# Where three kinds of products stand among the scores of a step: doubled sums, mixing values and the MLP output, in a six-layer attention stack

## Chip, cores and metric

The kernel runs on one core of a Trainium2 chip. The metric is the device time of one launch in microseconds (us), the median of several runs.

## What is computed

Eight sequences of 512 rows and 128 features go through a layer norm, six attention layers with weights of their own, and a gated feed-forward network. Cut to what matters:

```python
def layer(h, p):
    q = (h @ wq.T + bq).reshape(bh, sl, H, DH)      # H = 16 heads of DH = 8
    k = (h @ wk.T + bk).reshape(bh, sl, H, DH)
    scores = einsum('blhd,bmhd->bhlm', q, k) / sqrt(DH)
    w_avg = softmax(scores).mean(axis=heads)        # averaged over the heads
    new_w = softmax(w_avg + rel)                    # rel: decay with distance
    sa = einsum('blm,bme->ble', new_w, h)           # mixes the rows of h themselves
    h1 = ln1(h + sa); h2 = ln2(h1)
    ff = relu(h2 @ w1.T + b1) @ w2.T + b2
    return ln3(h2 + ff)
x = x + six_layers(layernorm(x))
x = x + gated_ffn(layernorm(x))
```

## The kernel before

A **unit** is one layer of one sequence; there are 48, walked in order (line 798). A unit has 32 **steps** (line 810), numbered through the whole run as s = 32 x unit + step. Each step makes two score tiles of 128x512: `scores` (line 436) issues two matmuls on TensorE (line 445), VectorE takes the negated maximum of each row (`top`, line 454), and ScalarE takes the exponential with the row's sum accumulated (line 461). Two steps make a `Group` of four score tiles; eight steps cover one block of 128 query rows (`lc`) with all sixteen heads.

Everything else is placed among the steps by a plan written by hand: `at(step, place, fn)` (line 653) puts a function into the list of a step and a place, `first` in front of that list, and the main loop (lines 798 to 824) takes them out in the order: the two scores, then the list PE_, the two maxima, the lists DVE_ and ACT_, the two exponentials, and last the list RING_. Each engine works its instructions in the order in which they are issued here. The other work, with its steps:

- **Doubled sums** (`gather`, matmul line 483): sixteen small matmuls add the exponentials of two groups, weighted by 1/sum (`weights`, line 468: a reciprocal on VectorE, the product `rp` on GpSimd), into the PSUM tile `acc`. Planned five steps behind the second of the two groups (line 748), which gives steps 0, 4, 8, 12 and so on, first in PE_. After every second of them ScalarE takes `w = exp(acc / 16)` (`mix_exp`, line 491).
- **Mixing**: three steps later `mix_turn` transposes w (line 217, tile pt_w) and VectorE multiplies by the decay (`mix_decay`, line 501); two steps after that `mix_values` (line 506) multiplies by h into `po`, and VectorE's `mix_end` (lines 517 and 518) divides and adds h into `z1`. These are steps 7 and 9 of each eight, that is 7, 15, 23, 31 and 1, 9, 17, 25.
- **Projections** of the unit after (`project_k` at step 3, `project_q` at step 5, line 702), hidden products of the MLP of the unit two before (`hidden`, steps 11, 13, 19, 21), and transposes of h and u (steps 27 and 29). `matmuls` (line 665) puts the product into PE_ and what empties it on ScalarE into ACT_ of the same step, in front of the exponentials.
- **MLP output** (`mlp_out`, line 398): two halves of sixteen recorded matmuls each, in RING_ of steps 30 and 38 (6 of the next unit); `mlp_add` on VectorE a step later; the third norm's statistics at 32, 40 and its end from 41 on. One unit near the end has steps 26 and 30 instead.

[...] six of the pool `ps_big` (tag "big", taken in turn by `ring`, line 179) for the score tiles and the MLP output; one for `acc`; and one, of the pool `ps_one` (tag "one", line 176), that pt_w, po, pk, pq, pf, pt_h and pt_u all take in turn. A buffer's next writer waits until the last reader of the tile before has done.

## Time and profile before

| what | value |
|---|---|
| median of 3 runs | 2744.67 us (2743.7 to 2747.99) |
| the profiled execution | 2744.88 us, its span 2743.1 us |
| granted TensorE clock | 0.997 |
| busy: PE, VectorE (DVE), ScalarE (ACT), GpSimd (POOL) | 95%, 90%, 91%, 66% |
| exponentials (line 461) | 3072, the first at 25.6 us, the last at 2518.4 us |
| one unit in the middle of the run | 51.84 us (1007.86 to 1059.70) |
| feed-forward tail behind the last unit | 223 us (2520 to 2743) |

The profile is of one execution. A line of its groups gives the source line, the engine, the operation, output<-inputs with their shapes, the count, then the busy time and the mean of one in ns, and behind the second bar the idle time of that engine just before such instructions with what ended it. A line of its waits reads "who waits <- for whom: us in total, times, the longest". A line of its timeline gives start and length in us, engine, line, operation and tiles; "x16" is a burst of sixteen, and brackets hold the idle time before it with its releaser. A wait that overlaps the tail of the instruction before it isn't booked as idle, so starts are compared as well.

### The profile page before, as it was taken

The numbers are of one execution on the slowest core, as the hardware profiler recorded it, in microseconds if no ns is written. First come the engines' busy times: TensorE is split into PE (matmuls) and PEld (weight loads), VectorE is DVE, ScalarE is ACT, GpSimd is POOL, SyncE is SP. The second block draws the span as 40 slices with busy tenths as digits, with TensorE's granted clock in tenths as the row PEclk, the third lists the DMA queues.
The fourth block names the chain that finished last, engine by engine and source line by source line (L and its number), as shares of the span: only waits on it lengthen the run. The fifth ranks groups of instructions, "written<-read, shape, count | busy, mean of one in ns | idle before, by whom it ended". The sixth has DMA issues, their size and how long they took to land.

```text
span 2743.1 us, 50487 instructions
## 1 busy us (share of the span) xinstructions
PE 2592.6 (95%) x14944; PEld 1422.5 (52%) x14944; DVE 2461.5 (90%) x5725; ACT 2509.0 (91%) x6846; POOL 1815.7 (66%) x1894
## 2 busy tenths in 40 slices
PE   6999999999999999999999999999999999998999
PEld 3444555554554554554554554555554454455787
DVE  6999999999999999999999999999999999998774
ACT  6999999999999999999999999999999999998443
POOL 5567667667667667667667667657666756765874
PEclk9999999999999999999999999999999999999999
DMA  6445444354354454444444444444444545441000
GB/s 145 110 109 125 95 111 104 89 115 116 91 116 99 93 116 111 99 113 93 103 109 108 108 105 96 108 103 114 108 99 108 124 108 127 113 108 39 8 24 17
DMA packets 135847, 273.67 MB, mean 100 GB/s; under 512 B 39696, under 2 KB 57232, under 8 KB 135568
## 3 DMA queue, kind: packets, MB, share of 16 engines
q1 hardware_dynamic: 133504, 269.31, 42.2%
q8 instruction: 121, 1.98, 0.3%
q10 hardware_dynamic: 2064, 1.08, 0.2%
q14 instruction: 158, 1.29, 0.1%
HBM read 13.86 MB, written 2.10 MB: 6 GB/s over the span
## 4 chain that ended last, share of the span: by engine, by line
ACT 47%; PE 28%; DVE 16%; issue 5%; POOL 4%; SPq 1%; DMA 0%; POOLq 0%; DVEq 0%; ACTq 0%
ACT e L461 40%; DVE top L454 10%; PE acc L483 7%; PE ps L445 7%; PE qh L569 4%; PE py L404 3%; ACT g L394 3%; ACT w L491 2%; PE pk L260 2%; PE po L509 2%; PE pq L269 1%; ACT uT L382 1%; PE fo L615 1%; PE q L569 1%; DVE z L518 1%
## 5 line engine op out<-in xcount | busy, mean ns | idle before, releaser
L461 ACT ACTIVATE e<-ps,top 128x512 f32<-128x512 f32 x3072 | 2088.2, 728 | 97.2 <-DVE top L454 72.7
L454 DVE TENSOR_REDUCE top<-ps 128x1 f32<-128x512 f32 x3072 | 1930.5, 679 | 181.7 <-PE ps L445 179.9
L445 PE MATMUL ps<-ks,qs 128*128 128x512 f32 x3040 | 1187.4, 471 | 46.1 <-ACT e L461 34.7
L445 PEld LDWEIGHTS ps<-ks,qs 128*128 128x128 f32 x3040 | 521.0, 189 | 653.9 <-ACT e L461 440.8
L461 ACT ACTIVATION_READ_ACCUMULATOR e<-ps,top 128x1 f32 x3072 | 757.4, 247 | 0.0
L483 PE MATMUL acc<-e,rp 128*32 128x512 f32 x6144 | 740.5, 600 | 5.0 <-POOL rp L472 5.0
L472 POOL TENSOR_TENSOR rp<-pick,r 128x256 f32<-128x256 f32 x384 | 236.3, 615 | 598.3 <-DVE rw L517 226.8
L483 PEld LDWEIGHTS acc<-e,rp 128*32 128x32 f32 x6144 | 160.5, 109 | 349.1 <-issue 323.3
L315 POOL TENSOR_TENSOR m<-hiq,mask 128x512 f32<-128x512 f32 x190 | 241.0, 1278 | 0.1
L315 POOL TENSOR_TENSOR m<-loq,mask 128x512 f32<-128x512 f32 x190 | 241.1, 1279 | 0.0
L392 PE MATMUL pf<-uT,w 128*128 128x512 f32 x384 | 203.4, 611 | 27.6 <-DVE z L518 27.5
L509 PEld LDWEIGHTS po<-h,wT 128*128 128x128 f32 x1536 | 201.8, 192 | 21.2 <-DVE wT L501 3.4
L404 PE MATMUL py<-w,g 128*128 128x128 f32 x1536 | 191.7, 278 | 21.3 <-ACT e L461 21.3
L509 PE MATMUL po<-h,wT 128*128 128x129 f32 x1536 | 203.6, 276 | 3.0 <-DVE wT L501 3.0
L404 PEld LDWEIGHTS py<-w,g 128*128 128x128 f32 x1536 | 179.6, 191 | 47.2 <-ACT e L461 44.2
L279 POOL TENSOR_TENSOR loq<-qT,hiq 128x512 f32<-128x512 f32 x48 | 61.6, 1282 | 212.1 <-DVE hiq L278 212.1
L394 ACT ACTIVATE g<-pf,b_col 128x512 f32<-128x512 f32 x192 | 135.6, 706 | 1.5 <-PE pf L392 1.1
L501 DVE TENSOR_TENSOR wT<-pt_w,decay 128x512 f32<-128x512 f32 x192 | 130.7, 681 | 0.0
L217 PE MATMUL pt_w<-ident,w 128*128 128x128 f32 x768 | 120.4, 279 | 7.6 <-ACT uT L382 0.2
L491 ACT ACTIVATE w<-acc 128x512 f32<-128x512 f32 x192 | 118.0, 614 | 2.6 <-PE acc L483 2.4
L217 PEld LDWEIGHTS pt_w<-ident,w 128*128 128x128 f32 x768 | 88.0, 140 | 47.5 <-ACT g L394 36.1
L392 PEld LDWEIGHTS pf<-uT,w 128*128 128x128 f32 x384 | 65.3, 189 | 70.5 <-PE ps L445 53.6
(115 smaller groups left out, 2516.4 us busy)
## 6 DMA issues: line engine op xcount, KB each, us to landing
qs<-m SPq DMA_DIRECT2D x1520, 128.0 KB, 2.4
ks<-hik SPq DMA_DIRECT2D x384, 64.0 KB, 2.0
ks<-lok SPq DMA_DIRECT2D x376, 64.0 KB, 2.0
rows<-in_rows SPq DMA_DIRECT2D x6, 448.0 KB, 4.9
x_in<-in_x SPq DMA_DIRECT2D x8, 256.0 KB, 3.0
fh<-square SPq DMA_DIRECT2D x8, 256.0 KB, 2.3
x_out<-in_x SPq DMA_DIRECT2D x8, 256.0 KB, 2.8
out<-y SPq DMA_DIRECT2D x7, 256.0 KB, 2.4
```

What stands on the lines that cost most here:

```text
L217: nc.tensor.transpose(pt[:, c * P : (c + 1) * P], src[:, c, :], ident)
L315: nc.gpsimd.tensor_tensor(m[:, lc - 2 * two], part.unsqueeze(2).to_broadcast([P, NB, PER_STRIP, QB]), mask.unsqueeze(1).to_broadcast([P, N ...
L392: nc.tensor.matmul(pf, w1[:, f * P : (f + 1) * P], self.uT, start=True, stop=True)
L394: return lambda: nc.scalar.activation(self.g[:, f, :], pf, AF.Relu, bias=cols["b1_col"][:, k : k + 1])
L404: nc.tensor.matmul(self.py[:, k, :], self.g[:, f, c * P : (c + 1) * P], w2[:, f, :], start=(f == 0), stop=(f == FC - 1),)
L445: nc.tensor.matmul(ps[s], qs[:, nb * P : (nb + 1) * P].bitcast(F32R), un.ks[:, i, :].bitcast(F32R), start=True, stop=True,)
L454: nc.vector.tensor_reduce(top[s], ps[s], AX.X, ALU.max, negate=True)
L461: nc.scalar.activation(self.e[:, nb, :], ps[s], AF.Exp, bias=top[s], accum_out=self.zs[:, i % 2, nb : nb + 1],)
L472: nc.gpsimd.tensor_tensor(self.rp.rearrange("p t n l -> p (t n) l"), pick.unsqueeze(1).to_broadcast([P, 2 * NB, QB]), r.rearrange("p t n - ...
L483: nc.tensor.matmul(acc[nb * QB : (nb + 1) * QB, :], self.rp[:, gr.turn % 2, nb, :], gr.e[:, nb, :], start=(gr.turn == 0), stop=(gr.turn == ...
L491: nc.scalar.activation(self.w.rearrange("p c l -> p (c l)"), acc, AF.Exp, scale=1.0 / H)
L509: nc.tensor.matmul(self.po, self.wT[:, c, :], self.unit.h[:, c, 0 : E + 1], start=(c == 0), stop=(c == LC - 1),)
```

## The change

`mlp_out` and `mlp_add` now work on one quarter (128 rows) instead of a half. `scores` takes a function that it calls between its two matmuls; the list BETWEEN_ of a step is taken out there, and RING_ is gone. Three things go into BETWEEN_: the doubled sums, at the same steps as before; the mixing values, one step later (2, 10, 18, 26), with `mix_end` behind the maxima of that step; and the quarters of the MLP output, at steps 27, 30, 31 and 39, each with its addition in DVE_ of the same step. The third norm's first statistics move from 32 to 33. Nothing is added to or taken from the sum of products.

```diff
-        def mlp_out(self, half):
+        def mlp_out(self, c):
             w2 = lay[self.d][2]
-            self.py = ring([P, 2, E], f"py_{self.n}_{half}")
-            for k in range(2):
-                c = 2 * half + k
-                for f in range(FC):
-                    nc.tensor.matmul(
-                        self.py[:, k, :], self.g[:, f, c * P : (c + 1) * P], w2[:, f, :],
-                        start=(f == 0), stop=(f == FC - 1),
-                    )
+            self.py = ring([P, E], f"py_{self.n}_{c}")
+            for f in range(FC):
+                nc.tensor.matmul(
+                    self.py, self.g[:, f, c * P : (c + 1) * P], w2[:, f, :],
+                    start=(f == 0), stop=(f == FC - 1),
+                )
...
-        def mlp_add(self, half):
-            part = self.z3[:, 2 * half : 2 * half + 2, :]
-            nc.vector.tensor_tensor(part, self.py, part, ALU.add)
+        def mlp_add(self, c):
+            nc.vector.tensor_tensor(self.z3[:, c, :], self.py, self.z3[:, c, :], ALU.add)
...
-        def scores(self, half):
+        def scores(self, half, between):
...
                     un.ks[:, i, :].bitcast(F32R),
                     start=True, stop=True,
                 )
+                if s == 0:
+                    between()
...
-    PE_, DVE_, ACT_, RING_ = range(4)
+    BETWEEN_, PE_, DVE_, ACT_ = range(4)
...
-        outs = (26, 30) if un.u == U - 3 else (30, 38)
-        for half, step in enumerate(outs):
-            at(s + step, RING_, lambda half=half: un.mlp_out(half))
-            at(s + step + 1, DVE_, lambda half=half: un.mlp_add(half))
-        norm_steps(s, un, un.norm_c, outs[0] + 2, outs[1] + 2, outs[1] + 3, 42, 43)
+        outs = (26, 27, 29, 30) if un.u == U - 3 else (27, 30, 31, 39)
+        for c, step in enumerate(outs):
+            at(s + step, BETWEEN_, lambda c=c: un.mlp_out(c))
+            at(s + step, DVE_, lambda c=c: un.mlp_add(c))
+        norm_steps(s, un, un.norm_c, 33, 40, 41, 42, 43)
...
-        first(s + 5, PE_, gr.gather)
+        at(s + 5, BETWEEN_, gr.gather)
...
-            at(s + 10, PE_, gr.mix_values)
-            at(s + 10, DVE_, gr.mix_end)
+            at(s + 11, BETWEEN_, gr.mix_values)
+            at(s + 11, DVE_, gr.mix_end)
...
-            peak, exps = gr.scores(half)
+            peak, exps = gr.scores(half, lambda: pending(s, BETWEEN_))
...
-            step_ring(s)
...
-    finish(U * PAIRS + 1)
+    finish(U * PAIRS + 2)
```

More of the change, by code (lines that the diff above doesn't have):

```diff
@@ L752, in plan_group @@
             at(s + 8, DVE_, gr.mix_decay)
-            at(s + 10, PE_, gr.mix_values)
-            at(s + 10, DVE_, gr.mix_end)
+            at(s + 11, BETWEEN_, gr.mix_values)
+            at(s + 11, DVE_, gr.mix_end)
     def step_rest(s):
-        pending(s, PE_)
-        pending(s, DVE_)
-        pending(s, ACT_)
-    def step_ring(s):
-        pending(s, RING_)
+        for place in range(4):
+            pending(s, place)
     for s in range(-2 * PAIRS, 0):
@@ L823, in attn_stack_then_ffn @@
             exps()
-            step_ring(s)
     plan_turns(U)
@@ L832, in finish @@
                 step_rest(s)
-                step_ring(s)
     def next_step():
@@ L838, in next_step @@
             step_rest(s)
-            step_ring(s)
     def done(b):
```

## The prediction

> **What bounds the kernel now.** I read the page's busy line and its costliest groups first, then the waits, then the timeline of one unit engine by engine. A unit is one layer of one sequence: 32 steps of two scores (128x512 each). I write 2.1 for the second score of step 2, G for a doubled sum (L483), V for mixing values (L509), M for the MLP output (L404), T for the transposes of w (L217), X for a projection or hidden product (L260, L269, L392).

> ```profile
> PE 2592.6 (95%) x14944; PEld 1422.5 (52%) x14944; DVE 2461.5 (90%) x5725; ACT 2509.0 (91%) x6846; POOL 1815.7 (66%) x1894
> ...
> L461 ACT ACTIVATE e<-ps,top 128x512 f32<-128x512 f32 x3072 | 2088.2, 728 | 97.2 <-DVE top L454 72.7
> ```

> Three engines look full. PE is not: matmuls overlap in the record, and PE's weight loads wait 452.2 us for ScalarE's exponentials. ScalarE sets the pace. Its start-to-start spacing, when fed, is 0.66 us per exponential (1003.72, 1004.38, 1005.05 in its timeline), 0.57 after g, kT or qT, 0.48 after w, 0.47 after hT, 0.66 after uT. One unit therefore needs 64 x 0.662 + 6 x 0.569 + 4 x 0.477 + 0.465 + 0.662 = 48.8 us. The unit that begins at 1007.86 lasts 51.84 us (the same exponential of the next unit starts at 1059.70): 3.0 us of starvation per unit, some 140 us in the run. That is all that a better order could gain.

> ```profile
> DVE top L454 <- PE ps L445: 179.9, 241, 6.7
> ...
> ACT e L461 <- DVE top L454: 72.7, 184, 1.9
> ...
> PE pf L392 <- DVE z L518: 27.5, 45, 1.3
> ```

> The chain is score on PE, maximum (top) on VectorE, exponential on ScalarE. The third line is the one to keep: po, pt_w, pk, pq, pf, pt_h and pt_u share ONE PSUM buffer (pool ps_one, tag "one", bufs=1), so X can't start until VectorE's z (L518) has read V's result. It bites already once per unit (45 times, 0.61 us).

> ```profile
> 1008.53 0.68 ACT L461 ACTIVATE e<-ps,top 128x512 f32<-128x512 f32 x1
> ...
> 1009.50 0.69 ACT L461 ACTIVATE e<-ps,top 128x512 f32<-128x512 f32 x1 [0.19 <-DVE top L454]
> ```

> A stall is read from starts: 0.97 instead of 0.66, so 0.31 lost, of which the page books 0.19. Read so, the unit loses 0.17, 0.31, 0.45 at steps 0, 1, 2; 0.28, 0.50, 0.72 at 8, 9, 10; 0.27 at 18 and at 26: each time behind G and V.

> ```profile
> 1002.60 2.05 PE L404 MATMUL py<-w,g 128*128 128x128 f32 x16 [0.49 <-ACT e L461]
> 1004.40 0.72 PE L445 MATMUL ps<-ks,qs 128*128 128x512 f32 x2
> 1004.96 0.60 PE L217 MATMUL pt_w<-ident,w 128*128 128x128 f32 x4
> 1005.32 0.47 PE L445 MATMUL ps<-ks,qs 128*128 128x512 f32 x1
> 1005.94 0.51 PE L445 MATMUL ps<-ks,qs 128*128 128x512 f32 x1 [0.15 <-ACT e L461]
> 1006.38 1.92 PE L483 MATMUL acc<-e,rp 128*32 128x512 f32 x16
> 1008.23 0.74 PE L445 MATMUL ps<-ks,qs 128*128 128x512 f32 x2
> 1008.81 1.05 PE L509 MATMUL po<-h,wT 128*128 128x129 f32 x8
> 1009.62 1.18 PE L445 MATMUL ps<-ks,qs 128*128 128x512 f32 x4
> 1010.74 1.10 PE L260 MATMUL pk<-hT,wqk 128*128 128x512 f32 x2
> ...
> 1024.46 1.10 PE L392 MATMUL pf<-uT,w 128*128 128x512 f32 x2 [0.52 <-DVE z L518]
> ```

> PE's order around a unit's start: M, two scores, T, two scores, G, two scores, V, four scores, X. The last line is the wait for z at step 11 (z starts at 1023.96, X 0.50 later).

> [...] in the lines above no score passes the waiting M (0.49) or pf (0.52). [...]

> **The change, part by part.** No product is added. Numbers used, all from this unit: scores follow each other by 0.23 on PE; a score after G ends 0.43 after G, after anything else 0.24; G ends 1.86, V 0.90, pk 1.05 after the end of the score before it; a maximum starts 0.04 after its score ends, maxima follow by 0.60; exponential 0.72 after the start of its maximum; rw 0.10 to 0.15 (I take 0.10), X 0.50 after the start of z; an evacuation 0.08 after its product ends (an estimate, twice the lag of top behind its score); a ring buffer is usable by PE 0.86 after the start of the exponential that reads it.

> *V, and what follows it.* Before: V behind 1.1, z behind top 1.1, X behind 3.1: four scores between V and X, and z two maxima ahead of those that X must outrun. After: V between 2.0 and 2.1, z behind top 2.1, X still behind 3.1: PE issues 2.1, 3.0, 3.1 and stands before X until top 2.0, top 2.1, rw and z are done. Queued behind X on PE: scores 4.0 and then G; on ScalarE, X's evacuation (kT, g, hT) stands ahead of exponentials 3.0 and 3.1, so it holds them too. In the shortest case (VectorE has nothing else): 2.1 ends at t, top t+0.04, rw +0.60, z +0.10, X +0.50, X done +1.10, evacuation +0.08 = t+2.42; exponential 2.1 is done at t+0.04+0.72+0.66 = t+1.42. ScalarE starves 1.0 us unless it has a backlog. This happens at steps 3, 11, 19, 27 (every V is followed by an X one step later): 0 to 4.0 us per unit.

> *G.* It moves one score earlier: 0.0 G 0.1. Then G and V have three scores between them, not two (good), X and T to the next G one, not two (bad). From the end of 0.0 to exponential 0.1: 1.86 + 0.43 + 0.04 + 0.72 = 3.05 us; ScalarE needs 4.6 exponentials in hand then, of at most six buffers.

> *M.* Four quarters of about 1.0 (half of 2.05) at 27, 30, 31, 39 in place of halves at 30, 38. Same matmuls, but four ring buffers per unit instead of two, and the quarter at 31 now stands with T and G within three scores. The adds: four narrower instead of two of 415 ns. Unseen form; between 0 and 0.7 us per unit more (two more at 351 ns, the z row's 128x128), I take 0.1, beside VectorE's 179.9 us of waits for scores. norm_c's first statistics move by a step, its end doesn't. DMA queues are not passed. POOL's rp (0.61) must be ready one score earlier for G: at step 4 it is done 1.3 us ahead, taken as nothing; without that cover at most 0.7 per G.

> *Sum.* I carried one unit in its new order through these intervals, each instruction starting at the later of its engine and its inputs. The start of a unit, with exponential 0.0 at 0: score 0.0 ends -1.51, G 0.35, 0.1 at 0.78, 1.0 1.01, 1.1 1.24, 2.0 1.47, V 2.37, 2.1 2.60, 3.1 3.06. Maxima 0.1 at 0.82, 1.0 1.42, 1.1 2.02, then r and statistics (0.60), 2.0 3.22, 2.1 3.82, rw 4.42, z 4.52; X 5.02 to 6.12. ScalarE: 0.1 at 1.54 (free at 0.66: 0.88 lost), 1.0 2.20, 1.1 2.86, 2.0 3.94 (0.41 lost), 2.1 4.60, kT 6.20 (free at 5.26: 0.94 lost); score 4.0 ends 6.35, G 8.21, w 8.29 (0.20 lost). With 0.46 at 0.0 (the quarter at 31 holds score -1.1 until -2.18, then the add and wT stand ahead of top 0.0) steps 0 to 4 lose 2.9 where they lose 0.9 now. The rest likewise: 8 to 14 lose 2.9 (now 1.5), 16 to 20 1.4 (0.3), 23 to 28 1.2 (0.3). Together 8.3 us per unit. The same reckoning for the order of now gives 2.55, at the very steps at which the trace loses 3.0; so I take the difference, 5.7 us. 44 full units (the first three and the last lack M, most X or both) x 5.7 + 4 x 1.5 = 257 us. The profiled execution took 2744.88 us (span 2743.1; median of the runs 2744.67): 2744.9 + 257 = 3002 us. The FFN tail (223 us) is untouched.

> **Rivals.** (1) *Only half the links bite.* ScalarE holds a backlog at steps 19 and 27, where it loses only 0.27 each now, and G's shift is neutral. Then 2 x 0.94 from steps 3 and 11 less some 0.4 from the wider G-V spacing: 1.5 per unit, 46 units, 69 us: 2814. Against it: in the order of now ScalarE is empty at 2, 10, 18 and 26 alike. (2) *Faster.* The wait for z is hidden everywhere, and G-V spacing counts: the losses at 1 and 9 (0.81) go and those at 2, 10, 18, 26 shrink by a score's time or so (0.7 together): 1.5 x 46 = 69 us less, 2676. It decides if ScalarE has 1.0 us or more in hand at exponential 2.1 of every group. For it: PE can be six scores ahead; against: G and V in between use that lead up. (3) *The edit changes nothing on PE.* The built order shows each product where the diff puts it, so this is nearly excluded; 2745.

> **Chances.** Forecast (2900 to 3060) 0.77; still slower, beyond 3060, 0.04; rival 1 (2780 to 2900) 0.10; rival 2 0.07; no change 0.02. Range 2870 to 3060: outside it lie rival 2, rival 3, the time beyond 3060 and some two thirds of rival 1, 0.20 in all. Faster by over 0.2% (about what this measurement can tell from no change) 0.07, within it 0.02, slower 0.91.

> **What would show it.** In the profile after: the wait of pf, pk and pt_h for z (L518's successor) grows from 27.5 us to well over 100; exponentials wait for top more than the 72.7, and g, kT, w wait for PE at all (now 1.1, 2.2, 2.4 us); unit length about 57.5 us; scores wait less for ScalarE than 452.2. Wrong if those X waits stay under 0.3 us each, or if the stall at the second score of step 0 is missing.

## The result, and the profile after

The changed kernel takes 3036.88 us (median of 4 runs, 3033.76 to 3042.83) against 2744.41 (4 runs): 1.1065 times as long, 95% interval 1.1043 to 1.1087. The profiled execution took 3039.68 us, its span is 3037.9 us, its mean granted TensorE clock 0.968 (0.997 before). The prediction was 3002, range 2870 to 3060.

The page of the changed kernel, lines as before:

```profile
PE 2649.5 (87%) x14944; PEld 1445.1 (48%) x14944; DVE 2474.4 (81%) x5821; ACT 2557.7 (84%) x6846; POOL 1811.9 (60%) x1894
...
L460 ACT ACTIVATE e<-ps,top 128x512 f32<-128x512 f32 x3072 | 2076.4, 700 | 136.6 <-DVE top L453 109.0
```

ScalarE's work is the same (6846 instructions in both); its share of the span fell from 91% to 84% because the span grew around it. The waits of the changed kernel (who waits <- for whom: us in total, times, longest):

```profile
DVE top L453 <- PE ps L442: 462.7, 373, 6.7
...
PE pf L392 <- DVE z L517: 187.9, 92, 2.9
...
ACT e L460 <- DVE top L453: 109.0, 263, 1.9
ACT w L490 <- PE acc L482: 98.9, 100, 2.5
PE pk L260 <- DVE z L517: 86.2, 46, 1.9
ACT g L394 <- PE pf L392: 68.2, 96, 3.7
...
ACT kT L261 <- PE pk L260: 41.5, 47, 2.2
...
PE pt_h L217 <- DVE z L517: 28.8, 42, 1.5
```

PE stands before pf, pk and pt_h until z has freed the shared buffer: 303 us, where it was 29 (27.5 before pf, 1.9 before pt_h). Behind that ScalarE waits for g and kT, which it hardly did, and VectorE for scores (462.7 for 179.9). One line is much larger than foreseen: w waits 98.9 us for the doubled sums, where the prediction's walk gives that wait 0.20 us per unit, some 10 us in the run.

A unit now takes 58.03 us, 6.19 more. TensorE's timeline around the start of the unit that begins at 1175.64 (start, length, and the idle time before it):

```profile
1174.00 1.93 PE L482 MATMUL acc<-e,rp 128*32 128x512 f32 x16
1175.86 1.20 PE L442 MATMUL ps<-ks,qs 128*128 128x512 f32 x4
1176.89 1.05 PE L508 MATMUL po<-h,wT 128*128 128x129 f32 x8
1177.70 0.94 PE L442 MATMUL ps<-ks,qs 128*128 128x512 f32 x3
1180.54 1.10 PE L260 MATMUL pk<-hT,wqk 128*128 128x512 f32 x2 [1.90 <-DVE z L517]
1181.07 0.79 PE L442 MATMUL ps<-ks,qs 128*128 128x512 f32 x1
1181.79 3.57 PE L482 MATMUL acc<-e,rp 128*32 128x512 f32 x16
1185.30 0.96 PE L442 MATMUL ps<-ks,qs 128*128 128x512 f32 x3
```

The same stretch on ScalarE:

```profile
1175.64 0.69 ACT L460 ACTIVATE e<-ps,top 128x512 f32<-128x512 f32 x1 [0.34 <-DVE top L453]
1177.12 0.69 ACT L460 ACTIVATE e<-ps,top 128x512 f32<-128x512 f32 x1 [0.71 <-DVE top L453]
...
1180.11 0.68 ACT L460 ACTIVATE e<-ps,top 128x512 f32<-128x512 f32 x1
...
1181.73 0.69 ACT L261 ACTIVATE kT<-pk,bk_col 128x512 f32<-128x512 f32 x1 [0.86 <-PE pk L260]
...
1185.44 0.60 ACT L490 ACTIVATE w<-acc 128x512 f32<-128x512 f32 x1 [1.68 <-PE acc L482]
```

Read from the starts, relative to 1175.64: exponential 0.1 at 1.48 (the prediction's walk: 1.54), X at 4.90 (5.02), kT at 6.09 (6.20), w at 9.80 (8.29). At these points up to kT the walk holds within 0.12 us. Then the doubled sums take 3.57 us instead of 1.92. The table of stretches (PE, PEld, DVE, ACT, POOL busy; granted clock; DMA share; GB/s) says why:

```profile
1178.38:1181.79 3.41, 1.51 (x5) 0.49 (x3) 3.17 (x9) 2.36 (x9) 3.25 (x4) 1.00 0.09 19
1181.79:1185.20 3.41, 3.41 (x17) 0.59 (x16) 0.69 (x1) 1.97 (x5) 1.04 (x1) 0.50 0.92 207
1185.20:1188.61 3.41, 3.41 (x20) 2.47 (x16) 2.78 (x6) 3.17 (x9) 0.61 (x2) 1.00 0.90 204
```

For 3.41 us TensorE was granted half its clock (0.50), right behind a stretch as long in which the wait for z left it busy for 1.51 us. DMA traffic doesn't tell the slow stretch from the one behind it, which has the full clock: its share is 0.92 in the one and 0.90 in the other. The trace has 53 such stretches among the 48 units (1 in the trace of before), 42 of them 6 us into a unit.

Folded over the 32 steps, ScalarE's losses in us in the middle of the run (start to start, less what a fed ScalarE needs; in the last column the median over the units for each step; the walk's figures are rounded as the prediction gives them):

| steps | before, trace | after, predicted walk | after, trace |
|---|---|---|---|
| 0 to 4 | 0.93 | 2.9 | 4.46 |
| 8 to 14 | 1.50 | 2.9 | 2.50 |
| 16 to 20 | 0.27 | 1.4 | 1.28 |
| 23 to 28 | 0.27 | 1.2 | 0.93 |
| sum | 3.0 | 8.3 | 9.2 |

### The profile page after: what moved, and what is told of

The parts are those of the page before. It is cut to its first block, busy times and chain, and to the rows that moved or that the text cites. A ratio compares the mean times of both kernels' runs of the same rounds, so it can differ in the third digit from the quotient of the medians.

```text
span 3037.9 us, 50373 instructions
## 1 busy us (share of the span) xinstructions
PE 2649.5 (87%) x14944; PEld 1445.1 (48%) x14944; DVE 2474.4 (81%) x5821; ACT 2557.7 (84%) x6846; POOL 1811.9 (60%) x1894
## 4 chain that ended last, share of the span: by engine, by line
DVE 44%; PE 41%; ACT 9%; issue 4%; POOL 1%; SPq 1%; DMA 0%; POOLq 0%; DVEq 0%; ACTq 0%
DVE top L453 33%; PE acc L482 19%; ACT e L460 7%; PE ps L442 6%; PE qh L568 4%; PE pf L392 3%; PE py L402 3%; DVE z L517 2%; DVE wT L500 2%; PE pk L260 2%; DVE st_c L194 1%; PE pt_w L217 1%; DVE r L469 1%; ACT uT L382 1%; PE pt_h L217 1%
## 5 line engine op out<-in xcount | busy, mean ns | idle before, releaser
L453 DVE TENSOR_REDUCE top<-ps 128x1 f32<-128x512 f32 x3072 | 1953.2, 677 | 462.9 <-PE ps L442 462.7
L442 PE MATMUL ps<-ks,qs 128*128 128x512 f32 x3040 | 1153.1, 466 | 13.7 <-ACT e L460 6.2
L482 PE MATMUL acc<-e,rp 128*32 128x512 f32 x6144 | 826.3, 660 | 1.6 <-POOL rp L471 1.3
L442 PEld LDWEIGHTS ps<-ks,qs 128*128 128x128 f32 x3040 | 532.4, 189 | 572.3 <-ACT e L460 405.8
L460 ACT ACTIVATION_READ_ACCUMULATOR e<-ps,top 128x1 f32 x3072 | 669.7, 218 | 0.0
L392 PE MATMUL pf<-uT,w 128*128 128x512 f32 x384 | 203.1, 610 | 187.9 <-DVE z L517 187.9
L482 PEld LDWEIGHTS acc<-e,rp 128*32 128x32 f32 x6144 | 169.6, 116 | 408.6 <-issue 336.9
L402 PE MATMUL py<-w,g 128*128 128x128 f32 x1536 | 211.9, 281 | 27.7 <-ACT e L460 23.1
L402 PEld LDWEIGHTS py<-w,g 128*128 128x128 f32 x1536 | 193.7, 191 | 70.4 <-ACT e L460 63.9
L490 ACT ACTIVATE w<-acc 128x512 f32<-128x512 f32 x192 | 114.9, 598 | 106.4 <-PE acc L482 98.9
L392 PEld LDWEIGHTS pf<-uT,w 128*128 128x128 f32 x384 | 64.9, 188 | 227.6 <-issue 218.9
L260 PE MATMUL pk<-hT,wqk 128*128 128x512 f32 x96 | 54.9, 655 | 87.1 <-DVE z L517 86.2
L217 PE MATMUL pt_w<-ident,w 128*128 128x128 f32 x768 | 120.4, 279 | 0.2 <-ACT uT L382 0.2
```

What stands on the lines that cost most here:

```text
L217: nc.tensor.transpose(pt[:, c * P : (c + 1) * P], src[:, c, :], ident)
L392: nc.tensor.matmul(pf, w1[:, f * P : (f + 1) * P], self.uT, start=True, stop=True)
L402: nc.tensor.matmul(self.py, self.g[:, f, c * P : (c + 1) * P], w2[:, f, :], start=(f == 0), stop=(f == FC - 1),)
L442: nc.tensor.matmul(ps[s], qs[:, nb * P : (nb + 1) * P].bitcast(F32R), un.ks[:, i, :].bitcast(F32R), start=True, stop=True,)
L453: nc.vector.tensor_reduce(top[s], ps[s], AX.X, ALU.max, negate=True)
L460: nc.scalar.activation(self.e[:, nb, :], ps[s], AF.Exp, bias=top[s], accum_out=self.zs[:, i % 2, nb : nb + 1],)
```

## The experiments

Theory A is the prediction's: the later place of the mixing values puts z two maxima later, X waits for it in the shared PSUM buffer, and ScalarE starves; the doubled sums' and the MLP's new places cost a little each. Theory B: the doubled sums' place is the price.

**The three parts, each alone.** Each is the kernel before with one part of the diff that stands above the prediction, and the hook between the scores that it needs.

Mixing values alone:

```diff
-            at(s + 10, PE_, gr.mix_values)
-            at(s + 10, DVE_, gr.mix_end)
+            at(s + 11, BETWEEN_, gr.mix_values)
+            at(s + 11, DVE_, gr.mix_end)
```

> The kernel before with one part of the change: mixing values between the two scores one step later, with their end a step later too. Theory A (the shared PSUM buffer: X waits for z, which now stands two maxima later): carried through the unit in this order, 3.8 us more per unit, 44 units, 2915 to 2935 us; if TensorE's clock is halved behind the wait at step 3 as in the changed kernel, some 70 us more, up to 2995. Theory B (the price is the doubled sums' place): 2745 to 2790.

Doubled sums alone:

```diff
-        first(s + 5, PE_, gr.gather)
+        at(s + 5, BETWEEN_, gr.gather)
```

> The kernel before with one part of the change: the doubled sums between the two scores. Theory A: X and T stand one score nearer to the next sums; 1.5 us more per unit, 46 units, about 2813 us (2785 to 2840). Theory B (this is the main price): 2940 or more.

MLP quarters alone:

```diff
-        outs = (26, 30) if un.u == U - 3 else (30, 38)
+        outs = (26, 27, 29, 30) if un.u == U - 3 else (27, 30, 31, 39)
...
+            at(s + step, BETWEEN_, lambda c=c: un.mlp_out(c))
+            at(s + step, DVE_, lambda c=c: un.mlp_add(c))
```

> The kernel before with one part of the change: the MLP output in quarters at 27, 30, 31, 39 between the scores. Theory A: 0.7 us more per unit, 44 units, about 2776 us (2755 to 2800). Theory B: as before, 2745. A third, that four ring buffers instead of two are the main price: above 2850.

**The changed kernel without the shared buffer.** The order of every engine is that of the change; only where po lies differs.

```diff
-            self.po = one([P, E + 1], f"po_{self.n}")
+            self.po = ring([P, E + 1], f"po_{self.n}")
```

> The changed kernel, its order untouched, but po takes a buffer of the ring of six instead of the single shared one, so X no longer waits for z. Theory A: the stalls at steps 3, 11, 19 and 27 go, PE no longer stands idle before X, and TensorE's clock isn't halved at step 4: 4.0 us per unit less by the reckoning and 1.6 us less for the clock, 2790 to 2850 us. Theory B (the doubled sums' place is the price): 2950 or more, since their place stays.

| kernel | us | ratio to before, 95% interval | unit, us (before 51.84) |
|---|---|---|---|
| mixing values alone | 2934.98 | 1.0691 (1.0673 to 1.0709) | 55.3 or 56.9 |
| doubled sums alone | 2778.72 | 1.0121 (1.0104 to 1.0138) | 52.52 |
| MLP quarters alone | 2765.96 | 1.0077 (1.0060 to 1.0094) | 52.47 |
| the change, po in the ring | 2774.40 | 1.0107 (1.0090 to 1.0123) | 52.55 |

Theory B falls: the doubled sums alone cost 34 us, and with their place kept but the link cut 262 of the 292 us are gone. Theory A holds, but two results lie outside its ranges: it put the doubled sums at twice their price (68 us expected, 2785 at the least), and the cut link at 2790 or more, 16 us above what came. The mixing values alone came at the top of their range (2935), with part of the price in the clock (0.984 granted, 0.997 before). With po in the ring, the same place in TensorE's timeline (that unit starts at 1073.68) shows pk right behind its scores, with no wait, and the doubled sums at their old length:

```profile
1076.66 0.50 PE L442 MATMUL ps<-ks,qs 128*128 128x512 f32 x1 [0.17 <-ACT e L460]
1077.00 1.02 PE L260 MATMUL pk<-hT,wqk 128*128 128x512 f32 x2
1077.46 0.80 PE L442 MATMUL ps<-ks,qs 128*128 128x512 f32 x1
1078.19 1.92 PE L482 MATMUL acc<-e,rp 128*32 128x512 f32 x16
```

Neither pf nor pk nor pt_h waits for z in that trace. The three parts alone cost 190, 34 and 21 us, 245 together; the change costs 292.

**The place of z in VectorE's queue.** The shared buffer stays, but `peak` takes a function that it calls between its two maxima, so z no longer stands behind both.

```diff
                 for s in range(2):
                     nc.vector.tensor_reduce(top[s], ps[s], AX.X, ALU.max, negate=True)
+                    if s == 0:
+                        middle()
...
-            at(s + 11, DVE_, gr.mix_end)
+            at(s + 11, MIDDLE_, gr.mix_end)
```

> The changed kernel with the end of the mixing (rw and z) between the two maxima of its step instead of behind both; po stays in the shared buffer. Theory A (X waits for z's place in VectorE's queue): one maximum of 0.60 less ahead of z, at four places, 2.25 us per unit by the reckoning and up to 1.6 for the clock: 2865 to 2940 us. Theory B (sharing the buffer costs by itself, wherever z stands): within 20 us of 3037.

Measured 2875.10 us (ratio 1.0467, 1.0449 to 1.0484), unit 54.16 or 55.79. So it isn't sharing the buffer as such: one maximum less ahead of z is worth 162 us, some of it clock, since the halved stretches among the units fall from 53 to 17 and the granted clock rises from 0.968 to 0.988.

**The clock.** The second score of step 3 of each unit is issued eight times into its tile, so that TensorE has work through most of its wait before pk.

```diff
+            warm = 8 if self.lc == 0 and i == 1 and half == 1 else 1
...
+                for _ in range(warm if s == 1 else 1):
```

> The changed kernel, with the matmul of the second score of step 3 of each unit issued eight times instead of once into the same tile (the result is the same), so that TensorE works through most of its wait for z in front of pk. Theory A (the doubled sums of step 4 take 3.57 instead of 1.92 us because TensorE's clock is halved for 3.41 us after it stood idle there): the halved stretches at step 6 us of a unit go, the unit falls from 58.0 to about 56.4 us, 42 units, about 2968 us (2955 to 3000, more if a halved stretch turns up at another step). Theory B (these sums are slow for another reason, their inputs or traffic of GpSimd and DMA at that time): 3037 or a little more.

Measured 3037.54 us (ratio 1.1065): nothing gained. That looks like theory B until its trace is read (the unit starts at 1174.05):

```profile
1178.95 1.10 PE L260 MATMUL pk<-hT,wqk 128*128 128x512 f32 x2 [0.26 <-DVE z L519]
1179.49 0.80 PE L444 MATMUL ps<-ks,qs 128*128 128x512 f32 x1
1180.21 1.92 PE L484 MATMUL acc<-e,rp 128*32 128x512 f32 x16
...
1193.68 1.10 PE L392 MATMUL pf<-uT,w 128*128 128x512 f32 x2 [2.49 <-DVE z L519]
1194.21 0.79 PE L444 MATMUL ps<-ks,qs 128*128 128x512 f32 x1
1194.94 3.59 PE L484 MATMUL acc<-e,rp 128*32 128x512 f32 x16
```

The sums of step 4 are back at 1.92 us, and the loss at step 4 fell from 1.83 to 0.16. But the halved stretch moved to the next long wait, before pf at step 11 (2.49 us; the granted clock is 0.50 from 1195.0 to 1196.6), and made the sums of step 12 slow, 3.59 us, in place of those of step 4 (the loss there rose from 0.22 to 1.90). So the filler was put at all four places:

```diff
-            warm = 8 if self.lc == 0 and i == 1 and half == 1 else 1
+            warm = (8, 10, 7, 4)[self.lc] if i == 1 and half == 1 else 1
```

> The changed kernel with the second score of steps 3, 11, 19 and 27 issued 8, 10, 7 and 4 times into the same tile (the result is the same), so that TensorE works through its waits for z at all four places, and not only in front of pk. Theory A (a halved clock costs one set of doubled sums per unit; with one wait filled it moved to the next): few halved stretches are left, the unit is about 56.4 us, 44 units, 2955 to 2985 us. Theory B (the halved stretch costs nothing on the whole, since other waits take its place): 3037.

Measured 2954.11 us (ratio 1.0761, 1.0743 to 1.0779), 1 us below the low end of the range, unit 56.36; the clock of the profiled execution:

```profile
core 0: 2953.3 us, clock 0.997
```

This settles it: 83 us of the 292 are the halved clock (granted 0.968 in the changed kernel, 0.997 here), which came with the wait for z and went when useless work filled it. Step by step ScalarE loses what it loses in the changed kernel, within 0.01 us (medians over the units), except at step 4, where the loss is 1.67 us smaller; so the filler itself costs nothing that can be seen. The sum of the parts fits too. Per unit the mixing values alone cost 3.5 us where no halved stretch falls into the unit (55.3) and 5.1 where one does (56.9), the other parts 0.68 and 0.63: 4.8 together, against 4.52 for the whole change with the clock kept. What the change costs beyond its parts is clock.

**Better orders.** First the kernel before, with the mixing values alone moved as above and po in the ring; then also the second MLP half at 39 between the scores instead of 38 behind them; then also the mask of q on VectorE at step 6 instead of 8.

```diff
-            at(s + step, RING_, lambda half=half: un.mlp_out(half))
+            at(s + step, BETWEEN_ if step == 39 else RING_, lambda half=half: un.mlp_out(half))
...
-        at(s + 8, DVE_, un.split_q)
+        at(s + 6, DVE_, un.split_q)
```

> The kernel before, with the mixing values between the scores one step later, and po in a buffer of the ring of six. Theory A: with the link to X gone the later place costs nothing, and doubled sums and mixing values stand three scores apart; the losses at steps 2, 10, 18 and 26 shrink, that at 8 grows: 0.3 us less per unit, about 2732 us (2722 to 2746). Theory B (the later place itself costs, through z1 and what follows): 2760 or more.

> As the run before it (mixing values between the scores, po in the ring), and the second half of the MLP output at step 39 between the scores instead of at 38 behind them, so that it no longer stands a step ahead of the transposes of w. Theory A: the loss at step 8 shrinks as well, 0.5 us less per unit than the kernel before, about 2722 us (2712 to 2740). Theory B: the half stands nearer to the doubled sums of step 8 and costs what it saves, 2732 to 2750.

> The fastest order so far (mixing values between the scores, po in the ring, second MLP half at 39), and the mask of q (hiq, 0.41 us on VectorE) at step 6 instead of 8, out of the stretch behind the doubled sums. Theory A: the loss of 0.94 at step 9 falls by the 0.33 of the mask: 0.3 us per unit, about 2691 us (2684 to 2702). Theory B (VectorE isn't what holds the maxima there): 2706 as before.

| kernel | us | ratio to before, 95% interval | unit, us |
|---|---|---|---|
| mixing values between, po in the ring | 2710.34 | 0.9871 (0.9855 to 0.9888) | 51.05 |
| and the second MLP half at 39 | 2705.74 | 0.9855 (0.9838 to 0.9871) | 50.93 |
| and the mask of q at step 6 | 2703.96 | 0.9852 (0.9836 to 0.9869) | 50.89 |

All three are faster than both kernels. The first came 12 us below the low end of what was expected, the second 6 us. In the first the losses at steps 2, 10, 18 and 26 went from 0.46, 0.72, 0.27 and 0.27 to 0, 0.26, 0 and 0, and that at step 8 grew from 0.28 to 0.55, as theory A had it. So the idea of the change, more score tiles between doubled sums and mixing values, does pay together with a ring buffer for po. How much of the 35 us the ring gives by itself isn't shown, since po in the ring with the mixing values at their old place was not run; at steps 3, 11, 19 and 27, where X waits for z, the kernel before loses nothing on ScalarE, which speaks for a small part.

The step from the first to the second is 4.6 us, the last 1.8, within their spread: the last run, expected at 2702 at the most, came where its theory B put it. Its theory A was right on step 9, where the loss fell from 0.94 to 0.63, but 0.26 came up at step 8. VectorE's groups show one reason. With the mask at step 8:

```profile
L278 DVE TENSOR_SCALAR hiq<-qT 128x512 int32<-128x512 int32 x48 | 19.7, 410 | 2.4 <-ACT qT L270 2.4
```

and with the mask at step 6:

```profile
L278 DVE TENSOR_SCALAR hiq<-qT 128x512 int32<-128x512 int32 x48 | 41.9, 872 | 4.7 <-ACT qT L270 4.7
```

It takes twice as long there. Within a unit it pushes the first maximum of step 7 back by 0.8 us, and the next three, to the end of step 8, by 0.3. What stretches the mask there was not shown.

## Why the prediction was right, point by point

*The bound.* ScalarE fed by TensorE through VectorE: right. All that was lost is ScalarE starving: its losses grew from 3.0 to 9.2 us per unit, and the unit by 6.19.

*Mixing values and X.* The mechanism and its size were right: 0.94 predicted at steps 3 and 11 with z's measured 0.50 to X, 0.98 and 0.92 found; X starts within 0.12 us of the walk. At steps 19 and 27 0.71 and 0.25 were found. Cutting the link took back 262 us, the clock's share included.

*Doubled sums.* The loss at the second score of step 0 is there (0.82 in the shown unit, 0.88 predicted). Alone the move was over-priced: 0.68 us per unit, not the 1.5 expected of that run. What each part costs depends on what the others leave: in the walk, too, the three alone (3.8, 1.5 and 0.7 by the expectations) didn't add to the whole, 5.7.

*MLP.* 0.63 us per unit alone against the 0.7 expected of that run. The unseen add of 128x128 takes 279 ns against 415 for twice the width, so four cost 0.29 us more per unit than two, between the bounds 0 and 0.7 and above the 0.1 taken. GpSimd's rp stayed in time, as assumed: in the shown unit it ends at 3.51 us and the sums start at 6.15, and in the whole run TensorE's sums stood idle for rp for 1.3 us (5.0 before), though their weight loads waited for it more often (102 times, 26.9 us, for 7 and 7.4).

*The sum.* 257 us were predicted and 292 came, and the nearness is partly luck: two terms were wrong in opposite ways. The term of 5.7 us per unit is too large: with the clock kept up it is 4.52 (56.36 less 51.84). The walk overshot the order of after (48.8 and 8.3, 57.1, for 56.36) and undershot that of before (48.8 and 2.55, 51.4, for 51.84), and I took the difference although I had seen that the second ran short. The term that was missing is the clock: "G 1.86" was taken from sums at the full clock, and "G 8.21, w 8.29 (0.20 lost)" became w at 9.80 and 1.83 lost. That is 1.67 us in nearly every unit, 83 us in the run. The four outer units were put at 1.5 each and cost 0.7, 1.2, 5.9 and 3.7; five units near the end cost 8.2 each. The tail, put at untouched, is 3.7 us shorter (221.0 us from the start of the last exponential, 224.7 before).

*Rivals.* Rival 1 fell because all four links bit: 0.98, 0.92, 0.71 and 0.25, though at step 27 it was near the truth: there most of the wait was covered. Rival 2 needed 1.0 us in hand at exponential 2.1; at step 3 ScalarE had far less (it starves at kT in the shown unit). It comes true in direction when the link is cut and the mixing values alone move (2710 measured, 2676 named). *What would show it:* the X waits, the unit length and the waits of g, kT and w came as listed; "scores wait less for ScalarE than 452.2" did so, but little (417.3).

## What to carry to other kernels

Where an engine works in order, as TensorE did here (the scores behind pk stood through its 1.90 us), don't price a moved product by its own length: ask which buffer its result holds, who frees it, how far back in that engine's queue the freeing instruction now stands, and what waits for the buffer. Here a product issued one score later, with its shared PSUM buffer freed two maxima later, cost 190 us by itself and 262 within the whole change, the clock included; with a buffer of a ring, the move by itself was a gain of 35. Then look at the granted clock behind the new wait (here 0.50 for 3.41 us in nearly every unit, 83 of the 292 us), and when a cure seems to do nothing, see whether the loss has only moved.

## What was not expected of the hardware

*The unit keeps step with this grid.* 17 lengths of 3.413 us are 58.02 us, and 35 units in a row of the changed kernel last 57.99 to 58.06 (58.03 on average), with the halved stretch 6.1 to 6.2 us into each; with the first filler they last 58.02 again although the slow sums are others. The five units near the end last 61.42 to 61.46, 18 lengths are 61.43. With the mixing values alone, at a granted clock of 0.984, one unit of 56.9 us follows on one or two of 55.3, with the halved stretch in the longer ones. That the halved stretch delays the unit until its next wait falls on the same part of the grid is my reading; it wasn't tried by itself. The price of one halved stretch alone makes the same sum (56.36 and 1.67 are 58.03), so chance is not excluded.
